# The last batch's cross-attention keys, projected in the front part for all key heads and kept in DRAM

## The chip, the cores and the metric

The kernel runs on one core of a Trainium2 chip. A core has a matrix engine (TensorE, PE in the profile, with its weight loads as PEld), a vector engine (DVE), an activation engine (ACT), a general engine (POOL) and a queue processor that mostly issues DMAs (SP). They run side by side and wait for one another through semaphores. The metric is device time in microseconds (us) of one execution; the lower, the better.

## The reference, cut to what matters

Two transformer layers over `x` of 4 batches, 256 tokens, 256 features, with a context `ctx` of 4 batches and 1601 rows. Layer 0 is self-attention, a masked attention over the context and a ternary feed-forward part; layer 1 a scan, a cross-attention and a mixture of experts. The change touches the cross-attention of layer 1 alone (16 query heads, 4 key heads of 128):

```python
kv_in = jnp.concatenate([context_hidden, draft_hidden], axis=1)
k = (kv_in @ Wk.T).reshape(bsz, total_len, KVH, HD)
v = (kv_in @ Wv.T).reshape(bsz, total_len, KVH, HD).transpose(0, 2, 1, 3)
k = _rms_norm(k, k_norm_w).transpose(0, 2, 1, 3)
...
k = _rope(k, full_position_ids)
...
scores = jnp.einsum('bhqd,bhkd->bhqk', q, k) * SCALE
probs = jax.nn.softmax(scores, axis=-1)
attn = jnp.einsum('bhqk,bhkd->bhqd', probs, v)
```

The kernel counts the 256 tokens first: chunks 0 and 1 of 128 keys are tokens, chunks 2 to 14 (thirteen, the last of 65 rows) are the context.

## The kernel before

**Two parts.** In the front part a loop of 97 trips (the variable `tick`) runs one Python generator per batch through layer 0 and the scan, and mixes other generators in between. Then the pair stage: 16 heads (batch, key head), each with two pairs of query heads, each pair with 8 steps of two key chunks. A step scores a chunk (`bsc`, L1309; read by ACT at L1310 and by DVE's running maximum `acc` at L1314), subtracts the maximum (DVE, L1331), takes the exponential (ACT, L1334), sums (POOL, L1346) and multiplies with the values (`bpo`, L1355). Steps of one pair are overlapped with the next pair's; into them are put, at numbered places, the preparation of the next head, the table of angles, the output projection (`bpw`) and the experts.

**Preparation of a head's keys** (`prep_kv`, one call for each group i of four chunks, called at four steps of the head before). It loads the group's context columns transposed (`cTk`, up to 512 KB, from the pool "db" of three buffers, L1226), multiplies each chunk with the head's 128 columns of the key weights into PSUM (`pk`, L1238: two matmuls of 128 columns, one for each half of the features), and, two chunks at a time, takes from PSUM the squares (ACT, L1149) and the products with the two rotary tables (DVE, L1150 and L1151: `ropek`, `ropuk`). `factor` adds the products crosswise (POOL, L1156), reduces the squares (DVE, L1158) and raises them to the power -1/2 (POOL, L1159); this factor `kn` is applied later, to the scores. Then the keys are transposed on PE (L1249) and copied to `kT` (ACT, L1251).

**Values made ahead** (`values_ahead`). The values of all four key heads of a context chunk are made in one go in the front part: the chunk against 512 columns of value weights (`vah`, L347), copied from PSUM to a staging tile (ACT, L350; tag "rope", three buffers, which `ropek` and `ropeq` also use), stored in DRAM (SP, L351). `tiles` loads a head's part back when the head is begun (L1183). There are two such generators: EARLY for batches 0 to 2, advanced at trips 2 to 33, and LATE for batch 3, one chunk a trip from trip LTICK = 80 on. LATE's weights lie in two buffers of the tag "sum", which hold values of batch 3's self-attention before and a pair's sum of exponentials afterwards. Each group's context tile comes from "db", which also serves `xcT` and `xct` of the masked attention, `cTk` and the experts' `wi`.

**Order.** The framework that turns this Python into one instruction stream for each engine keeps to the order of the Python text roughly: an instruction that is ready, with its buffers, can go ahead of earlier ones that are not. Buffers of a tag are given out in the order of the text. All loads and stores of the parts named here are issued by SP, in one stream.

Of the kernel before, what the change touches and what calls it, by code (L numbers as in the profile page):

```python
# [20 lines left out]
P = 128  # L21
# [13 lines left out]
TERN = 34  # L35
SIDE = 48
KEPT = 3
EARLY = tuple((b, i) for b in range(3) for i in range(4))
LATE = tuple((3, i) for i in range(4))
LTICK = 80  # L40
WTICK = 34
FILL = {t: 2 if t < 15 else 1 for t in range(2, 34)}
SIDEN = 2
# [72 lines left out]
def decoder_kernel(ctx: ExitStack, tc: tile.TileContext, at, t, out):  # L116
# [20 lines left out]
    def p1(name):  # L137

        ring[0] += 1
        if psb and ring[0] % 3 == 0:  # L140
            return psb[0].tile([P, 512], F32, tag="one", name=name, bufs=2)
        return psa.tile([P, 512], F32, tag="one", name=name, bufs=4)
# [25 lines left out]
    def db(name):  # L168

        return wk.tile([P, 1024], F32, tag="db", name=name, bufs=NDB)  # L170
# [136 lines left out]
    def w512(tag, name):  # L307
        return fr.tile([P, 512], F32, tag=tag, name=name, bufs=2 if tag == "ropu" else NROPE)
# [14 lines left out]
    def values_ahead(late):  # L323

        if late:
            wv = [fr.tile([P, 512], F32, tag="sum", name=f"wvl{c}", bufs=2) for c in range(2)]
        else:
            w = odd("w3", "wv")
            wv = [w[:, 512 * c : 512 * (c + 1)] for c in range(2)]
        for c in range(2):  # L330
            nc.sync.dma_start(
                out=wv[c].rearrange("p (g n) -> p g n", g=NKV),
                in_=t["wkv1"][c * P : (c + 1) * P].rearrange("p (g two n) -> p g two n", g=NKV, two=2)[:, :, 1, :],
            )
        for b, i in (LATE if late else EARLY):
            n, w = units(i)
            first = not (late or b or i)
            cT = db(f"vcT{b}{i}")[:, 0 : 2 * w].rearrange("p (c n) -> p c n", c=2)
            nc.sync.dma_start(out=cT, in_=t["ctxT"][b][:, i * 512 : i * 512 + w].rearrange("(c p) n -> p c n", p=P))
            kept_values[b, i] = dram.tile([n, P, 512], F32, tag=f"v{b}{i}", name=f"v{b}{i}")  # L340
            if first:
                yield
            for k in range(n):
                r = min(P, w - k * P)
                pv = p1(f"vah{b}{i}{k}")
                for c in range(2):
                    T.matmul(pv[0:r, :], lhsT=cT[:, c, k * P : k * P + r], rhs=wv[c], start=c == 0, stop=c == 1)  # L347
                nm = f"vst{b}{i}{k}"
                st = w512("rope", nm)
                A.copy(st[0:r, :], pv[0:r, :])  # L350
                nc.sync.dma_start(out=kept_values[b, i][k, 0:r, :], in_=st[0:r, :])  # L351
                yield


    def fw(name, k, n, eng, tag):
# [26 lines left out]
    def shared_weights():  # L382

        for w in (first_weights["wfc"], first_weights["wpj"]):
            nm = f"g{len(gam)}"
            w2 = w.rearrange("p c n -> p (c n)")
            part = sm([P, 1], "gpart", f"part{nm}")
            V.tensor_reduce(part, w2, AX.X, ALU.add, apply_absolute_value=True)
            pg = p1(f"pg{nm}")
            T.matmul(pg[:, 0:1], lhsT=cc("ones"), rhs=part, start=True, stop=True)  # L390
            gw = fr.tile([P, 1], F32, tag=nm, name=nm)
            V.tensor_scalar(gw, pg[:, 0:1], 1.0 / (FF * D), None, ALU.mult)
            hi = sm([P, 1], "ghi", f"hi{nm}")
            V.tensor_scalar(hi, gw, 1e-6, 0.5, ALU.add, ALU.mult)
            lo = sm([P, 1], "glo", f"lo{nm}")
            V.tensor_scalar(lo, hi, -1.0, None, ALU.mult)
            gam.append(gw)
            yield
            for i in range(2):
                wi = w2[:, i * 1024 : (i + 1) * 1024]  # L400
                neg = db(f"neg{nm}{i}")
                V.tensor_scalar(neg, wi, lo, None, ALU.is_lt)
                V.scalar_tensor_tensor(wi, wi, hi, neg, ALU.is_gt, ALU.subtract)
                yield
        hmr = fr.tile([P, 2, 16], F32, tag="hmr", name="hmr")
        nc.scalar.dma_start(out=hmr, in_=t["hmrep"])
        for c in range(2):
            V.tensor_mul(
                kron[:, c, :].rearrange("p (m d) -> p m d", d=16), hmr[:, c, :, None].to_broadcast([P, 16, 16]),
                cc("dmask")[:, None, :].to_broadcast([P, 16, 16]),  # L410
            )
        yield
# [637 lines left out]
    def before(b):  # L1050
        for stage in (self_attention, memory_attention, feed_forward, recurrence):
            yield from stage(b)
            if stage is self_attention:
                yield "attended"
# [11 lines left out]
    def run(gen):  # L1066
        for _ in gen:
            pass
# [77 lines left out]
    def rotate(src, ctab, stab, sq, r, u):  # L1146


        A.activation(sq[:, :, 0:HD1], src, AF.Square)  # L1149
        V.tensor_mul(r, src, ctab)  # L1150
        V.tensor_mul(u, src, stab)  # L1151
# [66 lines left out]
    def prep_kv(b, g, i):  # L1218

        d, e = bt[b], tiles(b, g)  # L1220
        nm = f"k{b}{g}{i}"
        n = min(4, NCH - 4 * i)
        k0 = max(0, 4 * i - 2)
        w = (4 * i + n - 2 - k0) * P
        cT = db(f"cT{nm}")[:, 0 : 2 * w].rearrange("p (c n) -> p c n", c=2)
        nc.sync.dma_start(out=cT, in_=t["ctxT"][b][:, k0 * P : k0 * P + w].rearrange("(c p) n -> p c n", p=P))  # L1226
        sq, r, u = rope_tiles(nm)
        for h in range(0, n, 2):
            m = min(2, n - h)
            pk = p1(f"p{nm}{h}").rearrange("p (c n) -> p c n", c=2)  # L1230
            there = [k >= 2 and (b, (k - 2) // 4) in kept_values for k in range(4 * i + h, 4 * i + h + m)]
            for q in range(m):
                k = 4 * i + h + q
                w = HD1 if there[q] else 2 * HD1
                for c in range(2):
                    o = (k - 2 - k0) * P
                    src = d["yT"][:, c, k * P : (k + 1) * P] if k < 2 else cT[:, c, o : o + P]
                    T.matmul(pk[:, q, 0:w], lhsT=src, rhs=e["wkv"][:, c, 0:w], start=c == 0, stop=c == 1)  # L1238
            ctab, stab = (a[:, 4 * i + h : 4 * i + h + m, :] for a in d["k"])
            rotate(pk[:, 0:m, 0:HD1], ctab, stab, *(a[:, h : h + m, :] for a in (sq, r, u)))  # L1240
            assert len(set(there)) == 1
            if not there[0]:
                A.copy(e["v"][:, 4 * i + h : 4 * i + h + m, :], pk[:, 0:m, HD1:256])

        factor(sq, r, u, n, nm, e["kn"][:, 4 * i : 4 * i + n])
        yield
        tp = p1(f"tp{nm}")
        for q in range(n):
            T.transpose(tp[:, q * P : (q + 1) * P], r[:, q, :], ident)  # L1249
        w = min(512, NKEY - 512 * i)  # L1250
        A.copy(e["kT"][:, 512 * i : 512 * i + w], tp[:, 0:w])  # L1251
# [251 lines left out]
    first = before_head(0, 0)  # L1503
    first_weights = {}
    tern = shared_weights()
    gens = [before(b) for b in range(B)]
    work = steps()
    through, tick, step, said = [False] * B, 0, 0, None
    while not all(through):
        for b, gen in enumerate(gens):  # L1510
            if tick >= START[b] and not through[b]:

                stage = (behind if b and tick < START[b] + 2 else next)(gen, "through")
                through[b] = stage == "through"
                if stage == "attended" and b == B - 1:

                    win = fw("win", D, 768, nc.sync, "w1")
                    wout = fw("wout", D, D, nc.sync, "rope")
                    second_part()
        for _ in range(FILL.get(tick, 0)):  # L1520
            (behind if tick < 6 else next)(ahead, None)
        if tick >= LTICK:
            next(late, None)
        if tick == WTICK:
            run(ahead)
            first_weights["wfc"] = fw("wfc", D, FF, nc.sync, "w3")
            first_weights["wpj"] = fw("wpj", FF, D, nc.sync, "w4")
        if tick >= TERN:
            behind(tern)
        if through[0] and psb:  # L1530
            if said != "first":
                said = next(first, "first")
            else:
                for _ in range(RATE):
                    if step < 8 and through[1 + step // 4]:
                        step = next(work) + 1
        elif tick >= SIDE and tick % SIDEN == 0 and said != "context":
            said = behind(first)
        tick += 1
    run(late)  # L1540
    run(first)
    run(work)
    assert not places, sorted(places)
# [72 lines left out]
```

## Time and profile before

| what | value |
|---|---|
| median of 3 runs | 1765.64 us (1764.61 to 1766.31) |
| the profiled execution | 1764.41 us |
| its span from the first instruction to the last | 1762.5 us |
| mean granted TensorE clock | 0.991 |
| moved between HBM and the core | 116.91 MB, 66 GB/s |
| `pk` from `cTk`, 832 records | busy 103.3 us |
| `vah` of batch 3, 48 full records | busy 23.0 us |

A record is one instruction as the profiler saw it. A float32 matmul shows as two records, each with its own weight load. Matmuls are pipelined: a record's duration overlaps the next one's, so the time that a group takes is read from the chain of waits, where pieces follow one another. In a group's line, the text ahead of the bar is line, engine, operation, output<-input, shapes and count; then come busy time and the mean duration in ns; then idle time of the engine ahead of these instructions and what ended it. In a table of stretches each row has the stretch, its length, and the busy time and count of each engine, then the granted clock of PE, the share of the DMA engines and their GB/s.

### The profile page before, as it was taken

The numbers are of one execution on the slowest core, as the hardware profiler recorded it, in microseconds if no ns is written. First come the engines' busy times: TensorE is split into PE (matmuls) and PEld (weight loads), VectorE is DVE, ScalarE is ACT, GpSimd is POOL, SyncE is SP. The second block draws the span as 40 slices with busy tenths as digits, with TensorE's granted clock in tenths as the row PEclk, the third lists the DMA queues.
The fourth block names the chain that finished last, engine by engine and source line by source line (L and its number), as shares of the span: only waits on it lengthen the run. The fifth ranks groups of instructions, "written<-read, shape, count | busy, mean of one in ns | idle before, by whom it ended". The sixth has DMA issues, their size and how long they took to land.

```text
span 1762.5 us, 20956 instructions
## 1 busy us (share of the span) xinstructions
PE 1697.8 (96%) x6792; PEld 986.5 (56%) x6792; DVE 1301.3 (74%) x2452; ACT 994.5 (56%) x1741; POOL 867.1 (49%) x719
## 2 busy tenths in 40 slices
PE   7899989988999999999999999999999999999998
PEld 4555668755555455454555555555555555555546
DVE  5663475788658778787787788787778778778776
ACT  2456653655456756566565556666555556656551
POOL 2210032211116677666776665576665656667551
PEclk9999999998999999999999999999999999999999
DMA  7321234201141111121211212031212213111102
GB/s 234 109 95 54 90 98 126 72 9 47 55 140 44 41 60 37 52 60 46 69 41 60 70 42 75 31 112 32 69 46 66 70 37 111 31 52 46 54 0 67
DMA packets 106565, 116.91 MB, mean 66 GB/s; under 512 B 9664, under 2 KB 80468, under 8 KB 106456
## 3 DMA queue, kind: packets, MB, share of 16 engines
q1 hardware_dynamic: 105160, 114.02, 20.8%
q10 hardware_dynamic: 1296, 1.54, 0.3%
q8 instruction: 55, 0.90, 0.2%
q14 instruction: 54, 0.44, 0.1%
HBM read 101.38 MB, written 14.16 MB: 66 GB/s over the span
## 4 chain that ended last, share of the span: by engine, by line
PE 71%; DVE 9%; ACT 8%; POOL 7%; issue 3%; DMA 1%; POOLq 0%; ACTq 0%; DVEq 0%
PE bpo L1355 18%; PE bsc L1309 18%; PE pk L1238 7%; POOL sum L1346 4%; PE vah L347 4%; PE mph L1013 3%; PE bpw L1385 3%; ACT s L1334 2%; ACT s L1310 2%; PE pq L1199 2%; PE xpo L700 1%; PE sc L536 1%; PE xsc L655 1%; PE mpe L1026 1%; POOL ropeq L1156 1%
## 5 line engine op out<-in xcount | busy, mean ns | idle before, releaser
L1346 POOL TENSOR_TENSOR sum<-sum,s 128x512 f32<-128x512 f32 (+1 forms) x411 | 533.3, 1298 | 84.8 <-ACT s L1334 59.0
L1309 PE MATMUL bsc<-qTb,kTb 128*128 128x512 f32 (+1 forms) x960 | 458.0, 597 | 5.6 <-ACT kTb L1251 5.4
L1355 PE MATMUL bpo<-s,vb 128*128 128x512 f32 (+1 forms) x960 | 459.4, 597 | 0.4 <-ACT s L1334 0.4
L1310 ACT ACTIVATE s<-bsc,kn 128x512 f32<-128x512 f32 (+1 forms) x480 | 317.3, 684 | 224.6 <-PE bsc L1309 202.3
L1314 DVE SCALAR_TENSOR_TENSOR acc<-bsc,kn,acc 128x512 f32<-128x512 f32 x448 | 332.6, 742 | 102.4 <-ACT s L1310 88.0
L1331 DVE TENSOR_TENSOR s<-s,bc 128x1024 f32<-128x1024 f32 (+1 forms) x256 | 288.9, 1141 | 15.4 <-PE bc L1327 15.3
L1334 ACT ACTIVATE s<-s 128x1024 f32<-128x1024 f32 (+1 forms) x256 | 256.5, 1006 | 54.9 <-DVE s L1331 53.4
L1309 PEld LDWEIGHTS bsc<-qTb,kTb 128*128 128x128 f32 (+1 forms) x960 | 173.7, 187 | 189.9 <-issue 131.5
L1355 PEld LDWEIGHTS bpo<-s,vb 128*128 128x128 f32 (+1 forms) x960 | 168.8, 191 | 138.8 <-issue 135.3
L1156 POOL TENSOR_TENSOR ropek<-ropek,ropuk 128x512 f32<-128x512 f32 (+1 forms) x64 | 76.9, 1202 | 179.6 <-DVE ropuk L1151 178.4
L1337 POOL TENSOR_TENSOR sum<-s 128x512 f32<-128x512 f32 x32 | 40.9, 1277 | 186.5 <-ACT s L1334 186.5
L1238 PEld LDWEIGHTS pk<-wkv,cTk 128*128 128x128 f32 x832 | 101.6, 192 | 9.3 <-issue 4.3
L1163 ACT ACTIVATE ropeq<-ropeq,rnq 128x128 f32<-128x128 f32 x128 | 41.2, 390 | 112.3 <-POOL rnq L1159 108.7
L1238 PE MATMUL pk<-wkv,cTk 128*128 128x128 f32 x832 | 103.3, 275 | 0.0
L347 PE MATMUL vah<-wv,vcT 128*128 128x512 f32 (+1 forms) x156 | 77.1, 630 | 4.3 <-DMA vcT<-in_ctxT 2.3
L1312 DVE TENSOR_SCALAR acc<-bsc,kn 128x512 f32<-128x512 f32 x32 | 24.0, 750 | 64.6 <-ACT s L1310 64.6
L1159 POOL TENSOR_TENSOR kn<-ssk,nhalf 128x4 f32<-128x4 f32 (+1 forms) x64 | 64.9, 1014 | 8.9 <-DVE ssk L1158 8.9
L1385 PEld LDWEIGHTS bpw<-wo,aT 128*128 128x128 f32 x256 | 48.5, 190 | 34.8 <-issue 20.8
L1156 POOL TENSOR_TENSOR ropeq<-ropeq,ropuq 128x512 f32<-128x512 f32 x32 | 43.8, 1369 | 47.5 <-ACT s L1310 35.6
L1149 ACT ACTIVATE squares<-pk 128x256 f32<-128x256 f32 (+1 forms) x128 | 46.9, 372 | 33.9 <-PE pk L1238 30.2
L1385 PE MATMUL bpw<-wo,aT 128*128 128x256 f32 x256 | 65.6, 379 | 0.3 <-ACT aT L1361 0.3
L268 POOL TENSOR_TENSOR rsr_xa<-rse_xa,nhalf 128x2 f32<-128x2 f32 x4 | 3.4, 853 | 125.9 <-DVE rse_xa L266 125.9
(501 smaller groups left out, 2533.7 us busy)
## 6 DMA issues: line engine op xcount, KB each, us to landing
cTk<-in_ctxT SPq DMA_DIRECT2D x32, 512.0 KB
v<-vst SPq DMA_DIRECT2D x48, 256.0 KB
vb<-v SPq DMA_DIRECT2D x48, 256.0 KB
wq<-in_wq SPq DMA_DIRECT2D x16, 512.0 KB
wo<-in_wo SPq DMA_DIRECT2D x16, 512.0 KB
wi<-in_wi SPq DMA_DIRECT2D x32, 256.0 KB
vcT<-in_ctxT SPq DMA_DIRECT2D x12, 512.0 KB
xcT<-in_ctxT SPq DMA_DIRECT2D x12, 512.0 KB
```

The source lines that it names most:

```text
L347: T.matmul(pv[0:r, :], lhsT=cT[:, c, k * P : k * P + r], rhs=wv[c], start=c == 0, stop=c == 1)
L1156: G.tensor_tensor(r4, r4, u4[:, :, ::-1, :], ALU.add)
L1159: G.tensor_tensor(rn, ss[:, 0:n], nhalf[:, 0:n], ALU.pow)
L1238: T.matmul(pk[:, q, 0:w], lhsT=src, rhs=e["wkv"][:, c, 0:w], start=c == 0, stop=c == 1)
L1309: T.matmul(pc[0:n, :], lhsT=e["kT"][:, k * P : k * P + n], rhs=q, start=True, stop=True)
L1310: A.activation(s[0:n, i, :], pc[0:n, :], AF.Copy, scale=e["kn"][0:n, k : k + 1])
L1314: V.scalar_tensor_tensor(self.acc[0:n, :], pc[0:n, :], e["kn"][0:n, k : k + 1], self.acc[0:n, :], ALU.mult, ALU.max)
L1331: V.tensor_tensor(s[0:n, 0:w, :], s[0:n, 0:w, :], self.bc[0:n, None, :].to_broadcast([n, w, 512]), ALU.subtract)
L1334: A.activation(s[0:n, 0:w, :], s[0:n, 0:w, :], AF.Exp)
L1346: G.tensor_tensor(self.sum[0:n, :], self.sum[0:n, :], s[0:n, i, :], ALU.add)
L1355: T.matmul(self.po, lhsT=e["v"][0:n, k, :], rhs=self.s[c][0:n, i, :], start=k == 0, stop=k == NCH - 1)
L1385: T.matmul(pw[:, j * 256 : j * 256 + 256], lhsT=aT[:, o : o + P], rhs=e["wo"][:, self.h + h, :], start=True, stop=True)
```

## The change

`keys_ahead` makes, after LATE's values and in the same way, the context keys of batch 3 for all four key heads: the chunk against 512 columns of key weights, a copy to a staging tile, a store in DRAM, one chunk a trip. What is stored is raw, without rotary and norm. LATE begins at trip 63 instead of 80, so it is written at trips 63 to 75 and the keys at 76 to 88. In `prep_kv` a batch with kept keys loads the head's part of the group (`raw`, from "db") instead of `cTk`; squares and rotary products read it from SBUF, for two chunks in group 0, four in groups 1 and 2, three in group 3, each in one instruction. Chunks 0 and 1, the tokens, are multiplied as before.

```diff
+KEYS = (3,)
-LTICK = 80
+LTICK = 63
...
+    kept_keys = {}
+
+    def keys_ahead():
+
+        wk4 = [fr.tile([P, 512], F32, tag="sum", name=f"wkl{c}", bufs=2) for c in range(2)]
+        for c in range(2):
+            nc.sync.dma_start(
+                out=wk4[c].rearrange("p (g n) -> p g n", g=NKV),
+                in_=t["wkv1"][c * P : (c + 1) * P].rearrange("p (g two n) -> p g two n", g=NKV, two=2)[:, :, 0, :],
+            )
+        for b in KEYS:
+            kept = dram.tile([NCH - 2, P, 512], F32, tag=f"k{b}", name=f"k{b}")
+            for i in range(4):
+                w = 512 if i < 3 else P
+                cT = db(f"kcT{b}{i}")[:, 0 : 2 * w].rearrange("p (c n) -> p c n", c=2)
+                nc.sync.dma_start(out=cT, in_=t["ctxT"][b][:, i * 512 : i * 512 + w].rearrange("(c p) n -> p c n", p=P))
+                for k in range(w // P):
+                    pk = p1(f"kah{b}{i}{k}")
+                    for c in range(2):
+                        T.matmul(pk, lhsT=cT[:, c, k * P : (k + 1) * P], rhs=wk4[c], start=c == 0, stop=c == 1)
+                    nm = f"kst{b}{i}{k}"
+                    st = w512("rope", nm)
+                    A.copy(st, pk)
+                    nc.sync.dma_start(out=kept[4 * i + k], in_=st)
+                    yield
+            kept_keys[b] = kept
...
-        cT = db(f"cT{nm}")[:, 0 : 2 * w].rearrange("p (c n) -> p c n", c=2)
-        nc.sync.dma_start(out=cT, in_=t["ctxT"][b][:, k0 * P : k0 * P + w].rearrange("(c p) n -> p c n", p=P))
+        done = 0
+        if b in kept_keys:
+            done = n if i else 2
+            raw = db(f"raw{nm}")[:, 0 : done * HD1].rearrange("p (c d) -> p c d", c=done)
+            nc.sync.dma_start(
+                out=raw, in_=kept_keys[b][k0 : k0 + done, :, g * HD1 : (g + 1) * HD1].rearrange("c p n -> p c n")
+            )
+        else:
+            cT = db(f"cT{nm}")[:, 0 : 2 * w].rearrange("p (c n) -> p c n", c=2)
+            nc.sync.dma_start(out=cT, in_=t["ctxT"][b][:, k0 * P : k0 * P + w].rearrange("(c p) n -> p c n", p=P))
         sq, r, u = rope_tiles(nm)
-        for h in range(0, n, 2):
+        if done:
+            o = n - done
+            ctab, stab = (a[:, 4 * i + o : 4 * i + n, :] for a in d["k"])
+            rotate(raw, ctab, stab, *(a[:, o:n, :] for a in (sq, r, u)))
+        for h in range(0, n - done, 2):
...
+    keys = keys_ahead()
...
-        if tick >= LTICK:
-            next(late, None)
+        if tick >= LTICK and next(late, "over") == "over":
+            next(keys, None)
...
     run(late)
+    run(keys)
```

## The prediction

> **What bounds the kernel now.** I read the page's busy times and slices first, then tables of busy time by stretch of the span, then the chain of waits and single lines.
>
> ```profile
> PE 1697.8 (96%) x6792; PEld 986.5 (56%) x6792; DVE 1301.3 (74%) x2452; ACT 994.5 (56%) x1741; POOL 867.1 (49%) x719
> PE   7899989988999999999999999999999999999998
> ```
>
> TensorE is the bound: 96% of the span, and from the twelfth slice on 9 tenths or more. The stretches (columns: PE, weight loads, DVE, ACT, POOL, clock, DMA share, GB/s) say where it is not:
>
> ```profile
> 50.00:100.00 50.00, 44.95 (x229) 25.12 (x228) 31.88 (x93) 27.80 (x62) 9.79 (x8) 0.97 0.34 112
> 100.00:150.00 50.00, 46.20 (x295) 26.72 (x294) 25.97 (x66) 27.65 (x71) 4.46 (x4) 0.93 0.23 76
> 150.00:200.00 50.00, 48.85 (x368) 28.49 (x367) 18.11 (x56) 34.79 (x95) 0.70 (x1) 1.00 0.20 67
> 340.00:440.00 100.00, 86.08 (x367) 59.41 (x366) 80.72 (x230) 52.39 (x76) 15.11 (x16) 0.93 0.12 36
> 440.00:540.00 100.00, 99.99 (x337) 53.09 (x335) 61.53 (x126) 55.66 (x102) 13.42 (x13) 1.00 0.27 88
> 1300.00:1700.00 400.00, 397.02 (x1464) 221.14 (x1463) 311.50 (x515) 232.60 (x384) 253.60 (x207) 1.00 0.18 56
> ```
>
> From 440 us on PE is never free (99.99 of 100, then 397 of 400), so the end is the PE work after 440 us and what little stalls it. Between 340 and 440 us it is free 13.9 us, and the clock granted there is 0.93, another 7 us: **20.9 us of PE lost** while DVE (80.7) and its chain with ACT lead. Counting instructions engine by engine against the code, trip 63 of the front loop opens at 340 us, trip 80 at 435, the last at 513.
>
> ```profile
> L347 PE MATMUL vah<-wvl,vcT x52: 592/592/697, 443.2 to 513.9; 128*128 128x512 f32 x48, 128*65 128x512 f32 x4
> L331 SPq DMA_DIRECT2D wvl<-in_wkv x2: 565/574/582, 247.8 to 248.4; - x2
> SPq L339 <- PE pk L1238: 59.0, 2, 47.4
> ```
>
> Batch 3's values (written at trips 80 to 92) run from 443 to 514 us, where PE is full. Their weights came at 248 us, as soon as their two buffers were free: the program is ordered by readiness too, not only by the place in the loop. What held the values back are the context tiles: the queue of SP waits 59.0 us for `pk` to free them, because three context loads of batch 0's first head took the three "db" buffers at 338 to 346 us.
>
> **PE work removed and added.** Two pieces of the chain of waits give the price of one group:
>
> ```profile
> 443.37 1.72 PE vah L347 x4
> 1624.48 1.78 PE pk L1238 x16
> ```
>
> A float32 matmul is two records. Removed: 13 chunks x 2 feature halves x 2 records x 4 heads = 208 `pk` records of 128 columns; 1.78/16 = 0.111 us each, 23.1 us, all in 1300 to 1650 us where PE is full. Added: 13 chunks of 4 records of 512 columns at 1.72 us, 22.4 us. **Net -0.8 us**: the same columns are streamed, only once for four heads instead of in four parts. By the groups' busy sums (103.3/832 and 23.0/48 us) it would be -25.8 + 24.9 = -0.9, so this term is safe.
>
> **Where the work lands.** This is the term that matters. The values move from trip 80 to trip 63, ahead of the three context loads, so their tiles can be loaded at about 338 us and their 22.4 us can lie in the 20.9 us that PE loses before 440 us; the keys (trips 76 to 88) take the values' old place. Upper bound of the gain 20.9; lower bound 0, if the chunks only push the front's own work back. The nearest rows are the stretches in which the other batches' values are made in the same way, 50 to 200 us: PE busy times clock is 43.6 + 43.0 + 48.9 = 135.4 of 150, 90%; in the last of them 98%. Today 340 to 440 has 86.08 - 7 = 79.1. At 90% that is 11 us won, at 98% 19; I take **15**.
>
> **ACT, SP and buffers in the front.** 13 more copies PSUM to SBUF at 0.59 us (28.2 us for 48) = 7.7 us of ACT, which is busy 52.4 of 100: hidden, and if that cover went, up to 7.7. SP gets 2 weight loads (0.57), 4 tiles (0.38) and 13 stores (0.32) to issue, 6.8 us of a queue that mostly waits.
>
> ```profile
> SPq L351 <- ACT vst L350: 44.5, 11, 9.7
> ```
>
> Each store waits on SP for its copy, and 13 more do. Behind them on SP stand the loads of `cTk`, `vb`, `wq`, `wo` for the first heads; in this stretch no wait of PE on a DMA shows, so they have time. New is one wait: the keys' weights use the two "sum" buffers of the values' weights, so their two loads (512 KB) start only after the last `vah`. 512 KB at the 374 GB/s that the busiest slice between 435 and 530 us reached is 1.4 us, the bound below is 0 (PE has the front's other matmuls, as no PE wait stands for the first ones), the bound above 8, from the first tile at the kernel's start (issued 5.3, used 13.3 us). I take 2. The keys' tiles and the first head's share "db", the staging tiles share "rope" with `ropek`; I price that within the 15.
>
> **The rotary from SBUF.** 16 context loads of batch 3 become 16 loads of raw keys (half the bytes, 0.83 against 1.66 MB per head; 0.50 us to issue as `vb`, against 0.37). The raw tile is freed by DVE instead of PE, later by one pair of multiplies.
>
> ```profile
> L1150 DVE TENSOR_TENSOR ropek<-pk,ctabk 128x256 f32<-128x256 f32 x112 | 46.8, 418 | 8.0 <-ACT squares L1149 4.7 <-DMA v<-vst 0.7
> L1150 DVE TENSOR_TENSOR ropeq<-pq,ctabq 128x512 f32<-128x512 f32 x32 | 21.9, 683 | 25.7 <-ACT squares L1149 24.8 <-DMA v<-vst 0.9
> L1120 DVE TENSOR_TENSOR ctabk<-ang,knw x4: 1151/1772/1774, 362.5 to 1337.1; 128x960 f32<-128x960 f32 x4
> L1343 DVE TENSOR_TENSOR rest<-rest,s x3: 1570/1642/1705, 1719.1 to 1722.6; 128x512 f32<-128x512 f32 x2, 65x512 f32<-65x512 f32 x1
> 715.00:735.00 20.00, 19.13 (x62) 8.93 (x61) 17.71 (x24) 12.02 (x20) 13.38 (x10) 1.00 0.20 66
> ```
>
> DVE per head now: 14 multiplies of 256 (0.42) and 2 of 128 (0.28), 6.4 us. After: 4 of 256, 4 of 512 (0.68), 2 of 384 (some 0.55), 5.5 us, if reading SBUF costs what reading PSUM does. It need not. The trace has DVE operations with both inputs in SBUF: `ctabk` takes 1.15 us at 362 us, when POOL is idle, and 1.77 us in the pair stage; `rest` takes 1.64 us for 512 columns beside POOL's sums, against 0.68 for 512 from PSUM, 0.96 more. The change makes 32 such multiplies (4 heads x 8), so 0 to 31 us more on DVE, which is free 88 of 400 us there. What reaches PE: four table operations begin in 715 to 735 us, and PE loses 0.87 us there against some 0.15 usual (3 of 400): 0.18 us each. 32 x 0.18 = 6; these are longer than the new ones, so I take **4**, bounds 0 and 31.
>
> The Trainium skill, page "SBUF — State Buffer", section "SBUF: two separate sides", says that a DVE operation with two SBUF inputs and a GpSimd operation reading SBUF take one shared port pair in turn, each for its whole length, the other standing still. Taken to the letter every multiply waits up to a whole sum of 1.30 us, an estimate of 42 us of DVE where the row gives 31; it speaks against this change, the trace agrees in direction, and the sum above does not use it.
>
> **Sum.** -0.8 - 15 + 2 + 4 = -9.8. The profiled run took 1764.4 us (span 1762.5 and 1.9 around it), so 1754.6; the median of the runs shown, 1765.6, lies 1.2 above it: **1756**. Its own range: 1744 (20.9 won, no stalls) to 1764 (11 won, 3 and 7 lost).
>
> **Rivals.** *Moved but not won, 1765:* DVE leads from 360 to 420 us, and a chunk of 1.72 us is longer than many of PE's gaps, so it delays the chain it is put between; 7 won, 7 lost. For it: PE's longest single wait between 335 and 530 us is 3.1 us. Against: loads and chunks no longer wait behind `cTk`.
>
> *Slower, the front stretches, 1775:* the end of the front is set by ACT and DVE, nothing is recovered, the 7.7 us of copies go on that chain and the weights' wait adds 3: -0.8 + 7.7 + 3 = +10. It decides once pair work does not fill PE behind the front. For it: staging tiles held by `ropek` and stores. Against: PE at 99.99% after 440 us, and ACT half idle.
>
> *Slower, the rotary stands still for POOL, 1785:* all 31 us reach PE in the last batch: -0.8 - 15 + 2 + 31 = +17, some +19 on the median. It decides if an `acc` (L1314) queued behind a held multiply frees its score bank after PE wants it. Against: 715 to 735 us, where PE kept running.
>
> That the change does not do what it says (batch 3's preparation still multiplying for chunks 2 to 14) I can't see in the code.
>
> **Chances.** 1756: 0.59. Not won: 0.15. Front stretches: 0.17. Held rotary: 0.08. Nothing moved at all: 0.01, counted as the same. A measurement here tells 0.2%, 3.5 us, from no change: faster 0.59, same 0.16, slower 0.25. The range that leaves out two in ten, the held rotary and the upper half of the stretched front above all, is 1744 to 1775.
>
> **What would show it.** Right: `vah` of batch 3 from about 342 us, PE in 340 to 440 at 90 or more with a clock nearer 1, `pk` from `cTk` down to 624 records, PE still full afterwards. Wrong: those stretches unchanged and the pair stage beginning later; or `ropek<-raw` multiplies well over 1 us with PE waiting for `acc` in the last batch; or PE waiting at the first key for its weights.

## The result, and the profile after

The changed kernel takes **1751.34 us** (median of 6 runs, 1750.18 to 1755.05) against 1765.57 us before: 14.2 us less, ratio 0.9924, 95% interval 0.9912 to 0.9936. The profiled execution took 1750.98 us with a span of 1749.1 us. The forecast was 1756.

The page's first lines, as before:

```profile
PE 1691.1 (97%) x6636; PEld 970.2 (55%) x6636; DVE 1302.7 (74%) x2428; ACT 998.2 (57%) x1741; POOL 877.0 (50%) x719
PE   7989989999999999999999999999999999999998
```

PE's busy time fell by 6.7 us only and the span by 13.4: half of what was won is time in which PE did nothing. Most of the other half is busy time that went at a higher clock: 0.93 to 1.00 in 340 to 440 us is 7 us. POOL, which got no new work, is 9.9 us busier; that is taken up below. The stretches of the changed kernel (columns as before: PE, weight loads, DVE, ACT, POOL, clock, DMA share, GB/s):

```profile
240.00:340.00 100.00, 93.37 (x433) 73.44 (x434) 70.99 (x148) 55.07 (x91) 37.38 (x28) 1.00 0.36 106
340.00:440.00 100.00, 97.43 (x388) 62.00 (x387) 75.52 (x209) 56.61 (x85) 14.64 (x13) 1.00 0.26 83
440.00:540.00 100.00, 99.87 (x354) 55.33 (x353) 64.21 (x140) 51.43 (x95) 14.93 (x15) 1.00 0.30 99
1300.00:1700.00 400.00, 393.72 (x1328) 208.63 (x1326) 324.09 (x508) 240.09 (x383) 269.17 (x214) 1.00 0.16 47
```

From 340 to 440 us PE was busy 86.08 at a clock of 0.93; now 97.43 at 1.00, so the 20.9 us that it lost there are 2.6. In the pair stage it is free a little more than before, 6.3 of 400 us instead of 3.0. The lines of the chunks, by tile, in the changed kernel:

```profile
L348 PE MATMUL vah<-wvl,vcT x52: 592/592/595, 358.7 to 423.1; 128*128 128x512 f32 x48, 128*65 128x512 f32 x4
L361 SPq DMA_DIRECT2D wkl<-in_wkv x2: 539/550/560, 422.9 to 423.8; - x2
L374 PE MATMUL kah<-wkl,kcT x52: 592/592/697, 429.1 to 506.5; 128*128 128x512 f32 x52
L1278 PE MATMUL pk<-wkv,cTk 128*128 128x128 f32 x624 | 77.4, 275 | 0.0
```

Batch 3's values now run from 359 to 423 us, the keys in the values' old place, and 208 `pk` records are gone. The keys' weights are issued when the last `vah` is through, and the first key comes some 6 us after that.

Where the time came from is best seen by following one kind of instruction that both kernels have 960 times. The start of the first `bpo` record of a head, as a difference to the kernel before (counted off the traces; a head has 60 records; the runs are those below):

```
first bpo of head     0      8     11     12     13     14     15   last bpo
the change          +5.7   +5.9   +6.1   +0.3   -4.0   -8.7  -13.7   -13.7
values63            -3.7   -3.6   -3.5   -3.5   -3.6   -3.5   -3.5    -3.5
keys_trip80        +25.1  +24.5  +26.4  +20.5  +16.2  +13.0   +8.1    +8.1
keys_unused         +4.3   +4.3   +4.1   +4.1   +4.1   +4.2   +4.1    +4.1
keys_first          +4.8   +5.1   +5.3   -0.6   -4.8   -9.6  -14.5   -14.5
rotary_from_psum    +5.3   +5.6   +4.8   -1.9   -7.6  -13.7  -18.6   -18.6
```

The front part became 5.7 us longer, though 22.4 us of PE work were added: 16.7 us of them lie in time that PE lost before. Nothing happens in heads 1 to 11. While the heads of batch 3 are prepared (during heads 11 to 14), 19.4 us are won.

### The profile page after: what moved, and what is told of

Its sections match the earlier page's. It is cut to its first block, busy times and chain, and to the rows that moved or that the text cites. A ratio compares the mean times of both kernels' runs of the same rounds, so it can differ in the third digit from the quotient of the medians.

```text
span 1749.1 us, 20626 instructions
## 1 busy us (share of the span) xinstructions
PE 1691.1 (97%) x6636; PEld 970.2 (55%) x6636; DVE 1302.7 (74%) x2428; ACT 998.2 (57%) x1741; POOL 877.0 (50%) x719
## 4 chain that ended last, share of the span: by engine, by line
PE 65%; DVE 12%; POOL 9%; ACT 9%; issue 4%; DMA 1%; POOLq 0%; ACTq 0%; DVEq 0%
PE bpo L1395 16%; PE bsc L1349 16%; PE pk L1278 5%; POOL sum L1386 5%; PE mph L1041 2%; PE bpw L1425 2%; PE vah L348 2%; ACT s L1374 2%; ACT s L1350 2%; DVE acc L1354 1%; PE xpo L728 1%; DVE s L1371 1%; PE pq L1227 1%; POOL ropeq L1184 1%; PE sc L564 1%
## 5 line engine op out<-in xcount | busy, mean ns | idle before, releaser
L1278 PEld LDWEIGHTS pk<-wkv,cTk 128*128 128x128 f32 x624 | 76.3, 192 | 8.3 <-issue 4.8
L1278 PE MATMUL pk<-wkv,cTk 128*128 128x128 f32 x624 | 77.4, 275 | 0.0
L351 ACT COPY vst<-vah 128x512 f32<-128x512 f32 (+1 forms) x52 | 30.3, 592 | 58.4 <-PE vah L348 20.6
```

## Experiments

Each was timed in five rounds beside the kernel before on the same chip, whose median was 1764.4 to 1765.0 us in these rounds. Times compared between experiments can come from different chips.

**Is it the values' move alone?** `values63` is the kernel before with one line changed.

```diff
-LTICK = 80
+LTICK = 63
```

> The kernel before with LTICK = 63 and nothing else: batch 3's values go to trip 63, no keys are made ahead. Theory A (the gain is PE's idle time before 440 us, filled by chunks): the front lost 20.9 us of PE in 340 to 440 us and the values are 22.4 us of PE work, so 13 to 19 us are won, about 1749 us, as fast as the change without any of its keys. Theory B (the gain needs the keys, that is the cheaper streaming in batch 3): within 3 us of 1765.6. Theory C (both parts are needed: the values leave a hole after 440 us that nothing else fills): PE in 440 to 540 us drops under 95 of 100, and 5 to 8 us are won.

Measured: 1761.59 us, ratio 0.9984 (0.9976 to 0.9993). A fell. The time is B's (2.8 us below the 1764.44 us of the kernel before in the same rounds), but what happens is C's: PE drops under 95 in 440 to 540 us, though less is won than C said. Its stretches, then PE's waits between 340 and 545 us (engine, line, what it waited for: us in total, times, the longest):

```profile
340.00:440.00 100.00, 97.85 (x389) 63.37 (x388) 75.95 (x211) 56.45 (x85) 14.96 (x13) 0.98 0.21 69
440.00:540.00 100.00, 90.56 (x333) 50.85 (x332) 71.32 (x149) 52.81 (x98) 19.33 (x18) 0.97 0.17 56
```

```profile
PE pc L866 <- DVE dtv L860: 4.6, 2, 2.6
PE pr L905 <- DVE cr L902: 1.8, 2, 1.5
PE pu L878 <- DVE el L875: 1.7, 2, 1.4
```

The values fill the first hundred us just as well, and a new gap opens in the second: 9.4 us and 3% of the clock. PE stands at the scan's matmuls (`pc`, `pr`, `pu`) for DVE. The scan of the last batch is a chain of small steps; what ran beside it before were the values.

**Are the keys alone enough?** `keys_trip80` is the changed kernel with `LTICK = 80`.

> The changed kernel with LTICK = 80: values at trips 80 to 92 as before, keys from trip 93 on, the rest at the loop's end. Theory A: nothing fills the idle 340 to 440 us, the keys' 22.4 us are added where PE is full and 19 to 20 us come back in batch 3: 1767 to 1771 us. Theory B: the gain stays, 1750 to 1755 us.

Measured: 1770.56 us, ratio 1.0023 (1.0011 to 1.0036): A by the median, and none of the twelve times is near B. They fall into two groups, five at 1764.7 to 1766.3 us and seven at 1770.5 to 1774.0, with a granted clock of 0.991 or 0.992 in the first and 0.988 to 0.990 in the second; the profile is of the second, and why there are two is open. In the table the front grows by 25 us for 22.4 us of work, and 18 us come back in batch 3 (26.4 to 8.1). In the profiles, values alone give -3.5, keys alone +8.1, both together -13.7: 18.3 us belong to neither part, but to having both. With the first group's 1.4 us above the kernel before in place of 8.1, and medians for the others, it would still be 12.7. The moved portion fills 340 to 440 us, and the new one the gap that it leaves.

**Does it matter what fills?** `keys_first` swaps the two generators.

```diff
-        if tick >= LTICK and next(late, "over") == "over":
-            next(keys, None)
+        if tick >= LTICK and next(keys, "over") == "over":
+            next(late, None)
```

> The changed kernel with the two generators swapped: keys at trips 63 to 75, values at 76 to 88. Theory A2 (any PE work that hangs on nothing fills the front's gaps; the gain is an interaction of moving one portion to 340 to 440 us and having a second one for 440 to 540 us): as fast as the change, within 2 us. Rival (the order matters, the values being needed first by nobody but the keys' weights waiting for the values'): 3 us or more away from the change.

Measured: 1750.96 us, 0.4 from the change. Which of the two comes first is all one; they are work that hangs on nothing.

**And if the keys are not used?** `keys_unused` makes and stores them in the front, but batch 3's heads multiply for their context keys as before, from `cTk`.

```diff
-        if b in kept_keys:
+        if b in kept_keys and b < 0:
```

> The changed kernel with its front part whole, values and keys, but batch 3's heads multiply for their context keys as before; the stored keys are not read. Theory (the front costs 5.7 us more than before and all of the rest is won in batch 3): 5 to 7 us slower than before, 1770 to 1772 us. Rival (the front as such is where the time is won): faster than before.

Measured: 1769.75 us against 1764.67 in the same rounds, 5.1 us more, ratio 1.0031 (1.0019 to 1.0043). The front costs 4 to 5 us on balance (4.1 in the table); the gain is cashed in batch 3.

**More of the same?** `keys_two_batches` has `KEYS = (3, 2)`.

> The changed kernel with the keys of batch 2 made ahead too (after batch 3's), 26 key chunks at trips 76 to 101, the last ones after the loop. Theory A: the idle time is used up, 22.4 us more go into a full PE and 19 to 20 us come back in batch 2: 1752 to 1756 us, 1 to 4 us slower than the change. Theory B: another 10 to 14 us faster, near 1738 us.

Measured: 1755.95 us, ratio 0.9948 (0.9936 to 0.9961), 4.6 slower than the change: A, which had said 1 to 4. Its first `bpo` comes 29.2 us later than before, 23.5 more than in the change for 22.4 us of PE work: there is no free time left. Batch 2's heads win 21 of that back.

**The keys' weights.** `key_weights_early`:

```diff
-        wk4 = [fr.tile([P, 512], F32, tag="sum", name=f"wkl{c}", bufs=2) for c in range(2)]
+        wk4 = [fr.tile([P, 960], F32, tag=n, name=f"wkl{n}")[:, 0:512] for n in ("ang", "sn")]
```

> The changed kernel with the keys' weights in the two buffers of the angle tables (free between batch 0's tables and batch 1's angles) instead of those of the values' weights, so that they can be loaded before the last values are made. In the changed kernel they were loaded at 423 us and the first key matmul came at 429 us, with 2.2 us of PE lost in 420 to 440 us. Theory A: that loss goes, 1 to 3 us faster than the change. Rival: the wait is covered, or the next wait (tile or staging) takes its place: within 1 us.

Measured: 1753.13 us, not faster than the change's 1751.34 (intervals of the ratio 0.9919 to 0.9943 and 0.9912 to 0.9936). PE in 340 to 440 us rises to 98.35, in 440 to 540 it falls to 99.52, and from head 1 on the run is 6 us behind the kernel before, like the change. Its weights were issued at 380 and 390 us instead of 423, and the first key came at 428.3 instead of 429.1 us: the one wait that the change added held the keys up by less than 1 us.

**When to begin.** `trip52` is the changed kernel with `LTICK = 52`.

> The changed kernel with LTICK = 52: values from trip 52, keys from 65, both done by trip 77. PE is free 6.6 us between 240 and 340 us in the changed kernel and 2.7 us between 340 and 540. Theory A2: up to 6 us can be won before 340 us, but the chunks run out before the scan's chain ends and a gap opens between 480 and 540 us as it did with the values alone (9.4 us there): between 2 us faster and 5 us slower than the change. Rival (earlier is simply better): 4 to 6 us faster.

Measured: 1766.75 us, 15.4 slower than the change, far outside both. Its stretches:

```profile
240.00:340.00 100.00, 92.57 (x407) 69.16 (x408) 62.01 (x123) 47.23 (x85) 34.37 (x27) 1.00 0.41 123
340.00:440.00 100.00, 99.24 (x396) 65.69 (x395) 69.41 (x199) 53.11 (x80) 12.63 (x13) 1.00 0.28 89
440.00:540.00 100.00, 89.56 (x324) 49.48 (x323) 67.21 (x160) 47.11 (x86) 13.53 (x13) 0.95 0.21 68
```

Nothing was won before 340 us (92.57 against 93.37), and the last key was made at 457 us, so the scan's end stood alone again: 10.4 us and 5% of the clock. The forecast had the gap but not its size, nor that the front's own work was put off by chunks that came too early: the last `xpo` of the masked attention starts at 363 us instead of the change's 347, the scan's last `pc` at 518 instead of 504.

**The rotary read from PSUM.** `rotary_from_psum` lets ACT copy each raw group to a PSUM tile and reads that; everything else is the change.

```diff
+            pr = p1(f"pr{nm}")[:, 0 : done * HD1].rearrange("p (c d) -> p c d", c=done)
+            A.copy(pr, raw)
-            rotate(raw, ctab, stab, *(a[:, o:n, :] for a in (sq, r, u)))
+            rotate(pr, ctab, stab, *(a[:, o:n, :] for a in (sq, r, u)))
```

> The changed kernel, but ACT copies each raw group from SBUF to a PSUM tile first and the squares and rotary products read that: 16 more ACT copies (some 0.6 us each, 9 us of an engine that is 60% busy) and 16 more PSUM tiles, and no DVE multiply with both inputs in SBUF. In the changed kernel 6 of the 32 multiplies were visibly held (0.96 to 1.52 us and the like), 3 us in all, while POOL's busy time grew by 9.9 us. Theory A (the standing still of DVE and POOL is small and mostly covered): within 2 us of the change, and the multiplies back at 0.68 us. Rival (it is what keeps batch 3 from winning its full 23.1 us): 3 to 4 us faster than the change.

Measured: **1745.98 us**, ratio 0.9893 (0.9879 to 0.9906), 5.4 faster than the change (4.8 if each is taken against its own kernel before) and the fastest of all: the rival, with more than it said. Groups by form, first of the change, then of this run (busy, mean ns | idle before):

```profile
L1178 DVE TENSOR_TENSOR ropek<-rawk,ctabk 128x512 f32<-128x512 f32 x8 | 7.1, 886 | 0.0
L1179 DVE TENSOR_TENSOR ropuk<-rawk,stabk 128x512 f32<-128x512 f32 x8 | 5.5, 685 | 5.3 <-POOL ropek L1184 2.9 <-POOL ropeq L1184 2.4
```

```profile
L1178 DVE TENSOR_TENSOR ropek<-prk,ctabk 128x512 f32<-128x512 f32 x8 | 5.4, 677 | 0.0
L1179 DVE TENSOR_TENSOR ropuk<-prk,stabk 128x512 f32<-128x512 f32 x8 | 5.4, 677 | 0.0
L1268 ACT COPY prk<-rawk 128x512 f32<-128x512 f32 x8 | 4.7, 590 | 0.0
```

The 5.3 us of idle time in the change's second line are DVE waiting for additions of POOL before it can write `ropuk`; with PSUM they are gone. The engines' busy times in this run, from its page, and the stretch of batch 3 (columns as before):

```profile
PE 1691.4 (97%) x6636; PEld 970.1 (56%) x6636; DVE 1299.9 (75%) x2428; ACT 1002.7 (57%) x1757; POOL 869.9 (50%) x719
1300.00:1700.00 400.00, 397.61 (x1340) 211.01 (x1339) 324.82 (x514) 248.94 (x403) 267.77 (x217) 1.00 0.15 47
```

With PSUM the multiplies are back at 677 ns and POOL at 869.9 us instead of 877.0. In the table batch 3 wins 23.4 us (4.8 to -18.6), all of its 23.1, instead of 19.8 of the changed kernel (6.1 to -13.7). The same shows in every run with one batch of keys: counted from head 11 to the end, 19.8 us with the raw keys read from SBUF in each of the change, `keys_first`, `trip52` and `key_weights_early` (18.3 in `keys_trip80`), and 23.4 with PSUM in this run and each of the three below. So the effect is not an accident of one order. The copy also frees the "db" tile earlier, which could be a cause of its own. The traces speak against it: after 1300 us neither profile shows a wait of PE, DVE, ACT or POOL on a DMA. PE is free 2.4 us between 1300 and 1700 us instead of 6.3, and its waits there name DVE and ACT. Which held multiply led to which of them was not followed.

**Trips around 63, with the rotary from PSUM.** `psum_trip60`, `psum_trip64` and `psum_trip67` differ from `rotary_from_psum` in `LTICK` alone.

> The same with LTICK = 60. With 52 the chunks ran out at 457 us and PE lost 10.4 us and some clock in 440 to 540 us, 15 us in all. Theory: with 60 a part of that gap opens, 2 to 6 us slower than with 63 (1746.0). Rival: no change within 1 us, or faster.

> The kernel with the rotary read from PSUM and LTICK = 64, one trip later than the fastest so far. With 67 the front's free PE time in 340 to 380 us came back (8.5 us slower), with 60 that after 500 us (9.5 us slower). Theory (both ends of the stretch must be covered, 26 chunks just do it): between the two, 0 to 4 us slower than 1746.0. Rival (a broad optimum between 61 and 66): within 1 us, or faster.

> The kernel with the rotary read from PSUM, and LTICK = 67: values at trips 67 to 79, keys at 80 to 92. Theory (the chunks are worth what they lie in: PE's free time between 340 and 540 us, which is longest in 360 to 440 and, without chunks, at the scan's end): the first chunks lie a little later, the last reach closer to the loop's end; 2 us faster to 3 us slower than the same with 63 (1746.0), as only 2.7 us of PE were left to win there. Rival (63 is a sharp optimum): over 4 us slower.

Measured: 1755.48, 1752.66 and 1754.54 us, against 1745.98 at 63. All three are worse than the theory: 67 is the rival (a sharp optimum), 60 and 64 are slower than theory and rival alike. The reason given holds, its size did not. First `psum_trip67`, then `psum_trip60`:

```profile
340.00:440.00 100.00, 92.20 (x371) 61.31 (x369) 76.10 (x210) 53.78 (x79) 12.97 (x13) 0.97 0.18 58
```

```profile
440.00:540.00 100.00, 93.15 (x325) 51.59 (x326) 59.56 (x135) 48.19 (x91) 13.66 (x13) 0.97 0.25 81
```

Begun four trips later, the first gap is back; begun three trips earlier, the last one is, each with a few per cent of the clock. Twenty-six chunks just reach from one to the other. For 64 the table's first column would read +8.1 instead of +5.3 us, and +9.6 from head 3 on; PE lost 1.7 us in 340 to 380 us there. The profiled executions differ by 4.3 us, as the column does; the medians differ by 6.7, and the rest of that is not accounted for.

**Both batches, rotary from PSUM.** `psum_two_batches`:

> The kernel with the rotary read from PSUM, and batch 2's keys made ahead too. Theory: batch 2's chunks find no idle PE in the front (22 us in, as in the run with two batches before), and with no multiply held by POOL its heads now win 23 to 24 us: 0 to 2 us faster than 1746.0. Rival (the longer front costs more than it did, or PSUM tiles run short): 2 us or more slower.

Measured: 1751.84 us, 5.9 slower than one batch: the rival. The first `bpo` comes 30.4 us later than before, 25.1 more than with one batch. Batch 2's heads win 21.5 us, but batch 3's only 19.0 where they won 23.4 alone. PE ran at 97.56 of 100 in 1500 to 1600 us, with 2.4 us of waits for the running maximum; why there is open (the profiled execution was 3 us above the median).

## Why the prediction was right

**PE work, -0.8 us:** right. 52 records came and 208 went, 24.8 us of busy time for 25.9; `keys_first` shows that the kind of chunk does not matter, `keys_unused` that the 22.4 us pay only by the 23.1 that they save.

**What the front wins, 15 us, and the weights' wait, 2:** right in kind, too small. Together 13 were forecast, and 16.7 measured (22.4 added, 5.7 longer). The lost PE time fell from 20.9 to 2.6 us, near the upper bound; the busy share of 50 to 200 us, from which I took the size, was too poor a model. The wait for the weights cost nothing that `key_weights_early` could take away. The 15 was picked between 11 and 19, and those rows could not decide between them.

**What held the values back:** the context tiles, I said, and this reading was wrong.

```profile
393.98 12.49 SPq L339 DMA_DIRECT2D vcT<-in_ctxT  x2
```

In the kernel before, the first two tiles were issued at 394 and 406 us and the first `vah` came at 443, soon after trip 80 opens at 435 by my count: not the tiles but their place in the loop held them. In the changed kernel the tile was issued at 339 us, as forecast, but the first `vah` came at 359 and not at about 342; until then PE was full with the front's own matmuls. No term of the sum rests on this reading.

**"The end is the PE work after 440 us":** right for the changed kernel, but only because the keys take the values' place. ("Never free" was too strong, too: between the stretches that I showed, from 540 to 1300 us, PE is busy 748.3 of 760 us before and 747.8 after.) I did not say that this is a condition, and so my first experiment missed by 12 us: without the keys, PE is free after 440 us as well. The idle time is not one gap at 360 to 440 us; it is a stretch from 340 to 540 us in which the front's chain leaves PE free wherever nothing else is at hand.

**The rotary from SBUF, 4 us:** right. Batch 3 won 19.8 us of 23.1, and reading PSUM wins the rest, 3.6 us by the table; by the medians the whole kernel gains 5.4. The bound of 31 us was far off: 6 of the 32 multiplies were stretched by more than 0.1 us, 2.8 us in all. Of the others, 10 ran while POOL ran nothing, and 16 ran beside an instruction of POOL without being held.

**Sum:** -9.8 forecast, -14.2 measured. The front is the term that was mis-sized, by some 4 us, and the rest agrees within 1.

**Rivals.** *Moved but not won* came true for the values alone (`values63`, -2.8 by the medians), by another way than I gave: not the chain was delayed, but the gap moved. *The front stretches* did not come true by its cause: no run shows copies of ACT that lengthen the chain. Where the front cost more than it won, in `keys_trip80` (+6.1 us by the medians), `trip52` (+1.8) and `keys_unused` (+5.1), it was chunks that lay in a full PE, a gap left open, or keys that were not read. *Held rotary* is real at an eighth (3.6 us of 31, by the table) to a sixth (5.4, by the medians) of its price; its own sum, +17, gives 1783 us and not the 1785 forecast.

## What to carry to other kernels

Work that waits for nothing is worth what it lies in: measure PE's lost time (idle and clock) along the whole stretch that it can be put in, and check that moving a portion does not open the gap that it filled until then. A portion moved won 2.8 us here, a portion added lost 6.1, and the two together won 14. When the added portion repeats work that is done later, its price is the PE time that finds no gap, 5.7 us here, and not its own 22.4. An operand brought to SBUF "for free" is not the same operand: here, where POOL sums all along, two SBUF inputs cost more than an extra copy to PSUM.

## What the runs showed of the hardware that I had not expected

POOL pays, too, for a DVE multiply with two inputs in SBUF. From the timeline of the changed kernel (start, duration), two places:

```profile
1371.72 3.93 POOL L1386 TENSOR_TENSOR sum<-sum,s 128x512 f32<-128x512 f32 x2
1373.18 0.41 DVE L1178 TENSOR_TENSOR ropek<-rawk,ctabk 128x256 f32<-128x256 f32 x1
1373.51 0.41 DVE L1179 TENSOR_TENSOR ropuk<-rawk,stabk 128x256 f32<-128x256 f32 x1
1373.85 0.68 DVE L1178 TENSOR_TENSOR ropek<-rawk,ctabk 128x512 f32<-128x512 f32 x1
```

```profile
1468.63 1.27 POOL L1184 TENSOR_TENSOR ropek<-ropek,ropuk 128x512 f32<-128x512 f32 x1
1468.96 1.49 DVE L1178 TENSOR_TENSOR ropek<-rawk,ctabk 128x512 f32<-128x512 f32 x1
1469.86 1.72 POOL L1386 TENSOR_TENSOR sum<-sum,s 128x512 f32<-128x512 f32 x1
```

In the first, two sums that take 1.28 us each otherwise took 3.93. The second one's record has 2.57: 1.29 more, about the 1.35 us from the start of the first multiply to the end of the third, while the multiplies ran at full speed. In the second the multiply's record looks as if it waited until POOL's addition ended, 0.94 us after its own start, ran on for 0.55, and POOL's next sum was 0.44 longer than usual. The Trainium skill, page "SBUF — State Buffer", section "SBUF: two separate sides", says that the two engines take a shared port pair in turn, whichever starts first, for the whole instruction. The second place agrees. In the first the multiply at 1373.18 starts 0.10 us after the record of POOL's second sum and still is not held, so the start of a record does not tell who comes first.
